# One TensorE operation for both matmuls of a scan step, and new places in the plan: a hybrid of state-space scan, convolution and attention on one core

## The chip, the cores and the metric

The kernel runs on one core of a Trainium2 chip. The metric is the device time in microseconds (us) of one execution, lower is better; the time of a kernel is the median of several runs. A separate execution was recorded by the hardware profiler, and all lines of "the profile" come from it.

## What is computed

The input x has 8 images of 384 channels by 32 x 32 pixels, so 1024 tokens each, in float32. Two layers follow each other. Cut to what matters:

```python
# layer 0: xn = rmsnorm(x); the same mamba runs forward and backward over the tokens
xz = xn @ in_proj.T;  u, z = split(xz)
u  = silu(causal_conv4(u) + b)
dt, Bm, Cm = split(u @ x_proj.T)              # rank 24, 16 states, 16 states
delta = softplus(dt @ dt_proj.T + bias)
h_t = exp(delta_t * A) * h_{t-1} + (delta_t * u_t) * Bm_t      # per channel, 16 states
y_t = sum_n h_t[n] * Cm_t[n] + D * u_t
g   = (y * silu(z)) @ out_proj.T                               # forward + backward
x   = x + res * (scale * g + sigmoid(depthwise3x3(xn)) * xn)
# layer 1, tokens of one image
t = t + attention(layernorm(t))               # 6 heads of 64, causal
t = t + gelu(layernorm(t) @ kron(..).T) @ kron(..).T           # 384 -> 1536 -> 384
```

The recurrence over h is most of the work: 384 channels x 16 states x 2 directions x 1024 tokens for each image.

## The kernel before

**The scan step.** A step handles 8 channels with their 16 states, which fill the 128 partitions, over all 1024 tokens in one direction. An image has 96 steps (`NSTEP`), eight images have 768. A step is made by `group` (L980). A DMA (L988) brings delta into a tile dA, with each channel's row repeated for its 16 states. ScalarE turns it into exp(delta*A) in place (L993). The 1024 tokens are two halves of 512, and for each half TensorE spreads delta*u over the 16 states with one bfloat16 matmul: 32 rows of the tile du3 against 32 rows of a fixed 0/1 matrix `dup` (L1002). The two halves lie in different groups of 32 rows. Each result fills one PSUM bank, a value named b. VectorE multiplies b by B in place (L1005) and runs the scan over dA and b (L1013), the second half continuing from the end of the first. GpSimd, called POOL, multiplies the state by C (L1016). `scans` (L916) lets TensorE sum two such steps over the states into a bank y, with eight records (`sums`, L950 to L959).

**Banks.** Of the eight PSUM banks, four ("psm") serve all other matmuls, three ("b") serve the scan input, and one ("y") collects the sums (`kinds`, L401). A b is free again when its scan has read it.

**The rest of the work.** For each image: `project` and `gates` make u and z, `prepare` and `deltas` make the convolution, B, C and delta, all ahead of the image's scans. Behind the scans come `local`, `finish`, `layernorm`, `attention`, `mix` and `forward`. In the middle of the run, an image's scans go on beside the preparation of later images and the attention and feed-forward of the image before.

**What sets the order.** The order on every engine is fixed before the launch by a planner, `Plan` (L105). Every operation is given with its engine, a cost in us, what it reads and writes, and a number `at`, its place. `run` (L170) plays the program through with these costs: the engine that can start earliest takes, of the operations that can start within 0.05 us of that moment, the one with the lowest place. The order found so is emitted; on the chip each engine works through its own queue strictly in it, and waits for what each instruction needs. So a place is a priority and not a time, and a cost that differs from the chip's shifts engines against each other.

- Values of kind "b" are handed out in order of place as banks come free; an operation that asks for two starts when it has both (`queue` and `hand_out`, L179 and L199).
- On ScalarE, operations whose function table is loaded are favoured by `STAY` (L247); another table costs a load, `ACT_TABLE_LOAD` in the profile. Ordinary transfers on SP wait until the planned DMA backlog is under `BACKLOG` (L238); loads with a place of their own, as the dA loads, do not.
- Scan operations get their place from the step's number, `HEAD` and `PERIOD` (L1397), with offsets: `LOAD` for the dA load, `DECAY` for the exponential, `PRODUCTS` for POOL's product, `SUMS` for y, `PARTS` for du3. The spread matmul's place, -1000 and up, comes ahead of nearly everything on TensorE.
- Other work gets places that run evenly over a window (`Window`, L446), given in periods (`PROJECT` to `FORWARD`) or in us for the first images (`PROJECT0` to `LAYER1`). Within it, VectorE and ScalarE operations that touch a psm bank are moved ahead by `EVICT`, transfers by `MOVE`.

In the profile all plain matmuls have line 331, that of the helper `mm`, so they are told apart by tile: b is the scan input, y the sums, pi the projection, pg the output projection, pk, pq and po those of attention, px and pw those of the convolutions and of B and C, s the scores. A float32 matmul leaves two records, a bfloat16 one leaves one.

Of the kernel before, what the change touches and what calls it, by code (L numbers as in the profile page):

```python
# [22 lines left out]
NH = L // HALF  # L23
# [17 lines left out]
KI, KO = 32, 12  # L41
# [38 lines left out]
def act(n):  # L80
    return 0.2 + n * 0.000833


def dve(n):
    return 0.07 + n / 940


def pool(n):
    return 0.1 + n * 0.0022
# [15 lines left out]
class Plan:  # L105
# [1 line left out]
    DRAIN = 0.19  # L107
    SLACK = 0.1
    SWITCH = 1.3
    STAY = 50.0  # L110
    BACKLOG = 50.0
    LANDING = 1.0
    DMA_LATENCY, DMA_RATE = 2.5, 262e3

# [4 lines left out]
    def op(self, engine, cost, fn, reads=(), writes=(), at=None, table=None, nbytes=0, holds=()):  # L119


        o = Op()
        o.engine, o.cost, o.fn, o.table, o.nbytes = engine, cost, fn, table, nbytes
        o.at = self.at if at is None else at
        o.placed = o.urgent = at is not None
        o.vals, o.allocs, o.users, o.ready, o.done = [], [], [], 0.0, None
        deps = set()

        def meets(a, b):
            return a is None or b is None or a == b  # L130

        for v in reads:
            v, part = v if isinstance(v, tuple) else (v, None)
            deps.update(w for w, q in v.writes if meets(part, q))
            v.reads.append((o, part))
            o.vals.append(v)
        for v in writes:
            v, part = v if isinstance(v, tuple) else (v, None)
            deps.update(w for w, q in v.writes if meets(part, q))
            deps.update(r for r, q in v.reads if meets(part, q))  # L140
            if part is None:
                v.writes, v.reads = [], []
            if v.kind is not None and v.left == 0 and v not in o.allocs:
                o.allocs.append(v)
            v.writes.append((o, part))
            o.vals.append(v)
        for v in holds:
            if v.left == 0 and v not in o.allocs:
                o.allocs.append(v)
            o.vals.append(v)  # L150
        deps.discard(o)
        o.vals = list(dict.fromkeys(o.vals))

        o.after, slot_of = [], set()
        for v in o.vals:
            v.left += 1
            if v in o.allocs:
                v.first = o
            elif v.first is not None and v.first not in deps:
                slot_of.add(v.first)  # L160
        for d in slot_of:
            d.after.append(o)
        o.waits = len(deps) + len(slot_of)
        for d in deps:
            d.users.append(o)
        o.index = len(self.ops)
        self.ops.append(o)
        return o

    def run(self):  # L170
# [55 lines left out]
        while len(order) < total:  # L226
            best = None
            for e in engines:
                cand = []
                for o in ready[e]:  # L230
# [6 lines left out]
                    if e == "SP" and not o.urgent:  # L237
                        t = max(t, dma - self.BACKLOG)  # L238
                    cand.append((max(t, free[e]), o))
# [5 lines left out]
                for t, o in cand:  # L245
                    if t <= t0 + 0.05:
                        a = o.at - (self.STAY if e == "ACT" and o.table in (None, table) else 0.0)  # L247
                        k = (a, o.index)
# [39 lines left out]
def conv_attn_hybrid_kernel(  # L288
# [41 lines left out]
    def mm(out_, lhsT, rhs, first=True, last=True):  # L330
        return nc.tensor.matmul(out_, lhsT=lhsT, rhs=rhs, start=first, stop=last)  # L331
# [6 lines left out]
    def half(hf):  # L338
        return slice(hf * HALF, (hf + 1) * HALF)
# [18 lines left out]
    dup = const.tile([P, P], BF16, name="dup")  # L358
# [51 lines left out]
    op = plan.op  # L410

    def dma(dst, src, reads, writes, nbytes, **kw):

        op("SP", 0.6, lambda: nc.sync.dma_start(dst(), src()), reads, writes, nbytes=nbytes, **kw)
# [18 lines left out]

    EVICT, MOVE, SUMS, PRODUCTS, DECAY, LOAD, PARTS = 111.21, 8.82, 26.97, -2.67, -328.02, -584.01, -478.49

    PROJECT, GATES, CONV, DELTA = (-1.521, -1.371), (-1.067, -1.026), (-0.976, -0.866), (-0.889, -0.365)
    LOCAL, OUTPUT, NORM, ATTEND = (0.661, 0.853), (1.005, 1.032), (1.082, 1.173), (1.202, 1.761)
    MIX, FORWARD = (1.787, 1.854), (1.855, 2.07)  # L440

    PROJECT0, EARLY, CONV0, DELTA0 = (-400.622, -296.945), (-523.036, 67.185), (-160.273, 70.933), (131.8, 263.184)
    GATES0, ZEROS, LATE, PROJECT1, GATES1 = (177.592, 252.86), (56.018, 117.713), (263.977, 276.95), (-19.453, 206.415), (352.446, 448.404)
    CONV1, DELTA1, LAYER1 = (250.186, 263.964), (271.922, 425.403), (675.476, 1110.704)

    class Window:  # L446

# [468 lines left out]
    def scans(b, t0, period):  # L916
# [14 lines left out]
        for a in range(NB):  # L931
            y = Val("y", [P, HALF], f"y_{b}_{a}")
            for d in range(2):
                step0 = (a * 2 + d) * GJ * BR

                du3 = Val("du3", [P, GJ, HALF], f"du3_{b}_{step0}", BF16)
                reads = [(dusd[d][s], (a // 2, k, hf)) for k in range(3) for hf in range(NH)]
                dma(
                    lambda t=du3: t.t,
                    lambda a=a, d=d: dusd[d][s].t[a * BR : (a + 1) * BR].rearrange(  # L940
                        "r h k (e j) t -> (r h k) e (j t)", j=GJ
                    ),
                    reads + [(dusd[d][s], ("z", hf)) for hf in range(NH)], [du3], P * GJ * HALF * 2, at=t0 + step0 * step_time - PARTS,
                )
                for j in range(GJ):
                    step = step0 + j * BR
                    at = t0 + step * step_time
                    hs = [group(b, a, d, j, r, at + r * step_time, du3, bcs[d]) for r in range(BR)]

                    def sums(y=y, hs=hs, d=d, j=j):  # L950
                        for hf in range(NH):
                            for r in range(BR):
                                q = hf * BR + r
                                mm(
                                    y.t[q * KI : (q + 1) * KI, :], sel[:, j].rearrange("p e i -> p (e i)"),
                                    hs[r].t[:, half(hf)], d == 0 and j == 0, d == 1 and j == GJ - 1,
                                )

                    op("PE", quad(HALF), sums, hs, [y], at=at - SUMS)  # L959
# [20 lines left out]
    def group(b, a, d, j, r, at, du3, bc):  # L980

        s = b % 2
        n = f"{b}_{a}_{d}_{j}_{r}"
        dA = Val("dA", [P, L], f"dA_{n}")

        rows = a * HC + r * KI
        src = ded[d][s].t[rows : rows + KI].rearrange("(e j) t -> j e t", j=GJ)[j]
        dma(  # L988
            lambda: dA.t, lambda: src.unsqueeze(0).to_broadcast([NS, GC, L]),
            [(ded[d][s], a // 2)], [dA], P * L * 4, at=at - LOAD,  # L990
        )
        g = (a * BR + r) * GJ + j
        op(  # L993
            "ACT", act(L) + 0.1, lambda: nc.scalar.activation(dA.t, dA.t, AF.Exp, scale=nA.t[:, g : g + 1]),  # L994
            [nA], [dA], at=at - DECAY, table=EXP,
        )
        rev = slice(None, None, -1) if d else slice(None)

        halves = [(hf, Val("b", [P, HALF], f"b_{n}_{hf}")) for hf in (range(NH - 1, -1, -1) if d else range(NH))]
        for hf, v in halves:  # L1000
            rr = slice((r * NH + hf) * KI, (r * NH + hf + 1) * KI)
            op("PE", 0.24, lambda v=v, rr=rr: mm(v.t, dup[rr, :], du3.t[rr, j]), [du3], [v], at=-1000.0 + at * 1e-3)  # L1002
        for i, (hf, v) in enumerate(halves):
            op(
                "DVE", dve(HALF), lambda v=v, hf=hf: nc.vector.tensor_mul(v.t, v.t, bc.t[:, 0, half(hf)]), [(bc, 0)], [v],  # L1005
                at=at,
            )

            def scan(v=v, hf=hf, first=i == 0):
                t = dA.t[:, half(hf)][:, rev]  # L1010

                h = 0.0 if first else dA.t[:, HALF : HALF + 1] if d else dA.t[:, HALF - 1 : HALF]
                nc.vector.tensor_tensor_scan(t, t, v.t[:, rev], h, ALU.mult, ALU.add)  # L1013

            op("DVE", 1.15, scan, [v], [dA], at=at)
        op("POOL", pool(L), lambda: nc.gpsimd.tensor_mul(dA.t, dA.t, bc.t[:, 1]), [(bc, 1)], [dA], at=at - PRODUCTS)  # L1016
        return dA
# [376 lines left out]

    PERIOD, HEAD = 393.0, 65.75  # L1397

    def stretch(span, b):
        return Window(span[0] * PERIOD, span[1] * PERIOD, HEAD + b * PERIOD)  # L1400
# [119 lines left out]
```

## Time and profile before

| | |
|---|---|
| median of 3 runs | 4003.02 us (3989.68 to 4006.04) |
| the profiled execution's own time | 4019.04 us |
| its span, first to last instruction | 4017.1 us |
| mean granted TensorE clock | 0.935 |
| instructions in the span | 54053 |
| first and last b matmul start | 151.4 us, 3742.7 us |
| moved by DMA | 858.92 MB, mean 214 GB/s |
| table loads on ScalarE | 226, 1283 ns each |

How to read it: PE is TensorE, PEld its weight loads, DVE VectorE, ACT ScalarE, POOL GpSimd, SP the engine that issues the transfers. A line of a group gives the source line, the engine, the operation, out<-in by tile, the shapes and the count; then busy us and the mean ns of one; then the engine's idle time just before, with what ended most of it. A line of waits reads: engine, tile and line, "<-", what released it, then total us, times, longest us. A timeline line gives start, duration, engine, operation and count.

### The profile page before, as it was taken

Reading aid. Unit: us, or ns where it says so; the run is one execution under the profiler, and the core shown is the slowest. Engines: PE = TensorE matmul, PEld = TensorE weight load, DVE = VectorE, ACT = ScalarE, POOL = GpSimd, SP = SyncE. Lnnn points to the kernel's source line nnn. Section 1 sums busy time; section 2 is a strip of 40 time slices with the busy share of each in tenths; the row PEclk is TensorE's granted clock in tenths of the full one; section 3 lists DMA queues with packets and bytes.
Section 4 is the critical chain, followed back from the end, with each engine's and each line's share of the span. In section 5 each row is a group of like instructions: output and inputs, shape, how many; then the busy total and the mean of one; then the engine's idle time right before and its main releaser. Section 6 shows DMA issues by size and latency. Waiting matters only on the chain.

```text
span 4017.1 us, 54053 instructions
## 1 busy us (share of the span) xinstructions
PE 3709.8 (92%) x17970; PEld 1404.8 (35%) x17970; DVE 3332.5 (83%) x4403; ACT 2825.4 (70%) x4468; POOL 2997.6 (75%) x2370
## 2 busy tenths in 40 slices
PE   7577879899999999999999999999999999999998
PEld 2111112443234432444224432444324432443363
DVE  1498979978988989889988999889998899999522
ACT  4756647776788857888678867888678867676364
POOL 1988877997579965899569975899669975776231
PEclk9677678899998999999999999989999999999998
DMA  7989997679976898769976799669986698578100
GB/s 249 270 243 262 255 258 218 178 225 239 270 213 179 236 238 259 205 187 251 269 232 199 226 253 285 190 185 255 260 242 194 181 255 240 147 192 218 49 20 25
DMA packets 301998, 858.92 MB, mean 214 GB/s; under 512 B 38312, under 2 KB 91576, under 8 KB 301720
## 3 DMA queue, kind: packets, MB, share of 16 engines
q1 hardware_dynamic: 301720, 855.47, 76.4%
q8 instruction: 143, 2.34, 0.3%
q14 instruction: 135, 1.11, 0.1%
HBM read 696.44 MB, written 160.68 MB: 213 GB/s over the span
## 4 chain that ended last, share of the span: by engine, by line
PE 53%; DVE 14%; DMA 10%; POOL 8%; issue 4%; ACT 2%; SPq 0%; POOLq 0%; DVEq 0%; ACTq 0%
DVE dA L1013 7%; PE b L331 7%; PE pc L331 6%; PE y L331 5%; PE pi L331 4%; DMA dA<-ded 4%; POOL dA L1016 4%; DVE b L1005 3%; PE t L1250 3%; PE s L331 3%; PE pk L331 3%; PE pvv L331 3%; PE pq L331 2%; DVE mx L1186 2%; POOL p L1240 2%
## 5 line engine op out<-in xcount | busy, mean ns | idle before, releaser
L1016 POOL TENSOR_TENSOR dA<-dA,bc 128x1024 f32<-128x1024 f32 x768 | 1806.1, 2363 | 605.0 <-DVE dA L1013 506.4
L1013 DVE TENSOR_TENSOR_SCAN dA<-dA,b 128x512 f32<-128x512 f32 x1536 | 1854.3, 1234 | 92.7 <-ACT dA L994 90.3
L1005 DVE TENSOR_TENSOR b<-b,bc 128x512 f32<-128x512 f32 x1536 | 996.9, 681 | 173.2 <-PE b L331 161.4
L994 ACT ACTIVATE dA<-dA,nA 128x1024 f32<-128x1024 f32 x768 | 863.4, 1145 | 272.3 <-DMA dA<-ded 234.0
L331 PE MATMUL b<-du,dup 32*128 32x512 bf16 x1536 | 609.4, 408 | 181.0 <-DVE dA L1013 158.8
L331 PE MATMUL y<-dA,sel 128*32 128x512 f32 x3072 | 489.2, 663 | 11.2 <-POOL dA L1016 8.3
L331 PEld LDWEIGHTS <-dup 32*128 32x128 bf16 x1536 | 132.9, 92 | 935.4 <-issue 903.0
L1186 DVE TENSOR_REDUCE mx<-s 128x1 f32<-128x512 f32 (+3 forms) x576 | 288.7, 547 | 186.1 <-PE s L331 182.3
L1240 POOL TENSOR_SCALAR p<-p,den 128x512 f32<-128x512 f32 (+3 forms) x576 | 327.1, 586 | 86.0 <-DVE den L1232 79.3
L1193 ACT ACTIVATE p<-s,mx 128x512 f32<-128x512 f32 (+3 forms) x576 | 329.4, 578 | 75.0 <-DVE mx L1186 74.1
L1257 ACT COPY pT<-t 128x512 f32<-128x512 f32 (+2 forms) x480 | 245.9, 546 | 129.2 <-PE t L1250 123.1
L331 PE MATMUL pi<-xp,win 128*128 128x512 f32 x576 | 312.4, 650 | 10.4 <-DVE xp L696 4.5
L1250 PE MATMUL t<-ident,p 128*128 128x128 f32 x1728 | 281.6, 298 | 29.7 <-POOL p L1240 14.0
L1456 ACT ACT_TABLE_LOAD x226 | 290.0, 1283 | 4.0
L331 PE MATMUL s<-k,q 64*128 64x512 f32 (+3 forms) x1152 | 283.7, 544 | 9.2 <-ACT p L1193 8.6
L1250 PEld LDWEIGHTS t<-ident,p 128*128 128x128 f32 x1728 | 200.1, 149 | 164.8 <-issue 74.0
L331 PE MATMUL pc<-pT,v 128*64 128x128 f32 x3456 | 251.0, 289 | 5.3 <-ACT pT L1257 4.9
L331 PEld LDWEIGHTS pc<-pT,v 128*64 128x64 f32 x3456 | 193.9, 142 | 100.5 <-ACT pT L1257 31.2
L913 POOL TENSOR_TENSOR u<-u,part 128x1024 f32<-128x1024 f32 x96 | 204.9, 2134 | 10.5 <-ACT part L905 9.9
L905 ACT CAST part<-u 128x1024 bf16<-128x1024 f32 x144 | 150.5, 1045 | 64.8 <-DMA dusd<-part 49.9
L1365 ACT ACTIVATE g<-ph 128x512 f32<-128x512 f32 x192 | 104.1, 595 | 118.4 <-PE ph L331 117.4
L331 PEld LDWEIGHTS y<-dA,sel 128*32 128x32 f32 x3072 | 75.4, 112 | 286.2 <-issue 152.6
(184 smaller groups left out, 4776.1 us busy)
## 6 DMA issues: line engine op xcount, KB each, us to landing
dA<-ded SPq DMA_DIRECT2D x768, 512.0 KB
ct<-urd SPq DMA_DIRECT2D x96, 513.5 KB
du<-dusd SPq DMA_DIRECT2D x96, 512.0 KB
xs<-xpd SPq DMA_DIRECT2D x96, 432.8 KB
dusd<-part SPq DMA_DIRECT2D x288, 128.0 KB
ded<-de SPq DMA_DIRECT2D x48, 512.0 KB
uz<-uzd SPq DMA_DIRECT2D x48, 512.0 KB
bc<-bcd SPq DMA_DIRECT2D x32, 512.0 KB
```

Source lines behind the costliest of these rows:

```text
L331: return nc.tensor.matmul(out_, lhsT=lhsT, rhs=rhs, start=first, stop=last)
L913: "POOL", pool(L), lambda part=part: nc.gpsimd.tensor_sub(du.t, du.t, part.t), [part], [du]
L994: "ACT", act(L) + 0.1, lambda: nc.scalar.activation(dA.t, dA.t, AF.Exp, scale=nA.t[:, g : g + 1]),
L1005: "DVE", dve(HALF), lambda v=v, hf=hf: nc.vector.tensor_mul(v.t, v.t, bc.t[:, 0, half(hf)]), [(bc, 0)], [v],
L1013: nc.vector.tensor_tensor_scan(t, t, v.t[:, rev], h, ALU.mult, ALU.add)
L1016: op("POOL", pool(L), lambda: nc.gpsimd.tensor_mul(dA.t, dA.t, bc.t[:, 1]), [(bc, 1)], [dA], at=at - PRODUCTS)
L1186: lambda sc=sc, g=g, w=k1 - k0, hh=hh: nc.vector.tensor_reduce(mx.t[:, g, hh : hh + 1], sc[hh].t[:, 0:w], AX.X, ALU.max, negate=True), [sc ...
L1193: nc.scalar.activation(ps[g].t[:, hh, 0 : k1 - k0], sc[hh].t[:, 0 : k1 - k0], AF.Exp, bias=mx.t[:, g, hh : hh + 1], accum_out=den.t[:, g, ...
L1240: nc.gpsimd.tensor_scalar(t, t, den.t[:, g, hh : hh + 1], 1.0, ALU.mult, ALU.mult)
L1250: nc.tensor.transpose(t.t[:, o + j * P : o + (j + 1) * P], ps[g].t[:, hh, j * P : (j + 1) * P], ident)
L1257: nc.scalar.copy(pT[g].t[:, hs[0] : hs[-1] + 1, 0:w], t.t[:, 0 : len(hs) * w].rearrange("p (h w) -> p h w", w=w))
L1456: nc.scalar.preload_act_table_set(table)
```

## The change

In `group`, the two matmuls that fill a step's two b banks were two planner operations of cost 0.24, each with one bank. They become one operation of cost 0.336 that issues both matmuls one after the other and takes both banks when it starts. It keeps its place. The readers on VectorE stay as they are.

All hand-set places and three of the planner's settings get other numbers: `STAY`, `BACKLOG`, the seven offsets, all windows, `PERIOD` and `HEAD`.

```diff
@@ class Plan
-    STAY = 50.0
-    BACKLOG = 50.0
+    STAY = 15.0
+    BACKLOG = 10.0
@@
-    EVICT, MOVE, SUMS, PRODUCTS, DECAY, LOAD, PARTS = 111.21, 8.82, 26.97, -2.67, -328.02, -584.01, -478.49
+    EVICT, MOVE, SUMS, PRODUCTS, DECAY, LOAD, PARTS = 27.83, 13.24, 12.22, -9.17, -222.27, -783.55, -339.2
-    PROJECT, GATES, CONV, DELTA = (-1.521, -1.371), (-1.067, -1.026), (-0.976, -0.866), (-0.889, -0.365)
-    LOCAL, OUTPUT, NORM, ATTEND = (0.661, 0.853), (1.005, 1.032), (1.082, 1.173), (1.202, 1.761)
-    MIX, FORWARD = (1.787, 1.854), (1.855, 2.07)
+    PROJECT, GATES, CONV, DELTA = (-1.525, -1.398), (-1.067, -0.985), (-0.952, -0.894), (-0.917, -0.358)
+    LOCAL, OUTPUT, NORM, ATTEND = (0.593, 0.969), (1.016, 1.081), (1.16, 1.227), (1.191, 1.755)
+    MIX, FORWARD = (1.81, 1.845), (1.879, 2.092)
-    PROJECT0, EARLY, CONV0, DELTA0 = (-400.622, -296.945), (-523.036, 67.185), (-160.273, 70.933), (131.8, 263.184)
-    GATES0, ZEROS, LATE, PROJECT1, GATES1 = (177.592, 252.86), (56.018, 117.713), (263.977, 276.95), (-19.453, 206.415), (352.446, 448.404)
-    CONV1, DELTA1, LAYER1 = (250.186, 263.964), (271.922, 425.403), (675.476, 1110.704)
+    PROJECT0, EARLY, CONV0, DELTA0 = (-373.152, -337.008), (-788.581, -96.07), (-84.26, 78.46), (50.858, 257.144)
+    GATES0, ZEROS, LATE, PROJECT1, GATES1 = (253.962, 443.889), (24.114, 455.177), (161.216, 306.444), (-92.709, 246.406), (452.944, 585.724)
+    CONV1, DELTA1, LAYER1 = (164.85, 479.335), (392.72, 578.245), (462.639, 791.646)
@@ def group
-        for hf, v in halves:
-            rr = slice((r * NH + hf) * KI, (r * NH + hf + 1) * KI)
-            op("PE", 0.24, lambda v=v, rr=rr: mm(v.t, dup[rr, :], du3.t[rr, j]), [du3], [v], at=-1000.0 + at * 1e-3)
+
+        def spread():
+            for hf, v in halves:
+                rr = slice((r * NH + hf) * KI, (r * NH + hf + 1) * KI)
+                mm(v.t, dup[rr, :], du3.t[rr, j])
+
+        op("PE", 0.336, spread, [du3], [v for _, v in halves], at=-1000.0 + at * 1e-3)
@@
-    PERIOD, HEAD = 393.0, 65.75
+    PERIOD, HEAD = 418.62, 167.66
```

## The prediction

> **What bounds the kernel now.** I read the page's busy line and its costliest groups first, then busy time by stages, then VectorE's waits, then single stretches of TensorE's timeline.
>
> ```profile
> PE 3709.8 (92%) x17970; PEld 1404.8 (35%) x17970; DVE 3332.5 (83%) x4403; ACT 2825.4 (70%) x4468; POOL 2997.6 (75%) x2370
> ...
> L1013 DVE TENSOR_TENSOR_SCAN dA<-dA,b 128x512 f32<-128x512 f32 x1536 | 1854.3, 1234 | 92.7 <-ACT dA L994 90.3
> L1005 DVE TENSOR_TENSOR b<-b,bc 128x512 f32<-128x512 f32 x1536 | 996.9, 681 | 173.2 <-PE b L331 161.4
> ...
> L331 PE MATMUL b<-du,dup 32*128 32x512 bf16 x1536 | 609.4, 408 | 181.0 <-DVE dA L1013 158.8
> ```
>
> The matmul that the change pairs is 609 of TensorE's 3710 us. Its reader, the product and the scan on VectorE, is the largest work of that engine: 2 x (0.681 + 1.234) = 3.83 us for each of the 768 steps.
>
> By stages (the span cut where the scans start, at 151 us, end, at 3745 us, and in eight equal parts between, one for each image):
>
> ```profile
> core 0: us, PE busy (x) PEld busy (x) DVE busy (x) ACT busy (x) POOL busy (x), PEclk, DMA share, GB/s
> 151.00:600.00 449.00, 333.54 (x1065) 68.54 (x1067) 390.92 (x453) 258.85 (x272) 386.01 (x188) 0.69 0.93 260
> ...
> 1948.00:2397.00 449.00, 435.40 (x2231) 168.34 (x2231) 408.78 (x535) 348.90 (x554) 369.95 (x291) 0.99 0.83 233
> ...
> 3295.00:3745.00 450.00, 428.42 (x2168) 160.98 (x2168) 438.31 (x575) 297.06 (x487) 300.13 (x253) 0.98 0.72 189
> 3745.00:4017.00 272.00, 253.66 (x1334) 127.81 (x1333) 73.82 (x145) 131.23 (x331) 59.10 (x147) 0.96 0.09 32
> ```
>
> Four kinds of stretch: the first image is held by transfers (DMA share 0.93, TensorE only 74% busy), the six in the middle by TensorE (97%), the last image's scans by VectorE (97%), and the tail by TensorE alone. Over the six middle images (600 to 3295 us, 449.2 each) TensorE is busy 2591 us and VectorE 2411: 432 and 402 an image.
>
> Whether a busy TensorE is a full one has to be asked. The Trainium skill (Perfetto Trace Analysis, Identifying the Most-Contended Engine) holds that matmul busy time is a bad measure, and that weight-load busy share is a better one. By that, the middle windows stand at 168/449 = 37%, TensorE has room, and the change would give next to nothing. I checked by start times instead: between 600 and 3295 us, all time by which two matmul starts lie further apart than 0.54 us sums to 107 us, 4%. Its queue issues almost without pause. Here the trace decides: TensorE is the bound, and what an instruction costs is the distance it puts between its neighbours' starts.
>
> **What a lone matmul costs.** Two stretches of TensorE's timeline:
>
> ```profile
> 2000.40 1.12 PE L331 MATMUL pg<-yg,wout 128*128 128x512 f32 x2
> 2001.45 0.39 PE L331 MATMUL b<-du,dup 32*128 32x512 bf16 x1
> 2001.77 1.98 PE L331 MATMUL pg<-yg,wout 128*128 128x512 f32 x4
> 2003.69 0.39 PE L331 MATMUL b<-du,dup 32*128 32x512 bf16 x1
> ```
>
> ```profile
> 1876.40 1.07 PE L331 MATMUL pw<-xs,wl__13047 96*32 96x512 f32 x8
> 1877.40 0.39 PE L331 MATMUL b<-du,dup 32*128 32x512 bf16 x2
> 1877.72 1.07 PE L331 MATMUL pw<-xs,wl__13047 96*32 96x512 f32 x8
> ```
>
> In the first, every b sits alone; the next instruction starts 0.32 us after it, and the stretch before it is longer too. Where a lone b stands between two matmuls of one kind, their starts are 0.84 us apart (pi, pg, pk, po, pq, px: 208 cases), and without it 0.43 (pg, pk, po, px) or 0.53 (pi, pq). So a lone b costs 0.31 to 0.41 us; I take 0.36. In the second stretch two b's stand together: they share one 0.39 us and the next starts 0.32 us after. Their rows differ, and the second starts 3 to 37 ns after the first. A second b beside the first is nearly free. Of 1377 runs of b's, 1291 have only one, and only 27 neighbours start together.
>
> **The change, part by part.**
>
> *The pair.* 768 - 27 = 741 lone matmuls go from TensorE's path: 741 x 0.36 = 267 us (230 to 304 at the ends). An image has 96 steps, so TensorE falls from 432 to about 432 - 741/8 x 0.36 = 399 us, level with VectorE's 402, whose work does not change. So VectorE takes over, and the gain is counted from its idle time.
>
> ```profile
> DVE mx L1186 <- PE s L331: 94.7, 80, 8.2
> DVE dA L1013 <- ACT dA L994: 81.9, 35, 11.1
> DVE b L1005 <- PE b L331: 57.7, 74, 3.3
> DVE x L1319 <- PE po L331: 12.0, 12, 3.0
> ```
>
> These are VectorE's waits over the six middle images (total us, times, longest). TensorE's lateness is the first, third and fourth, with smaller ones 175 us, 29 us an image. ScalarE's and the transfers' lateness is 82 + 17 = 99 us, 16.5 an image, which the pair doesn't touch.
>
> *What remains of TensorE's lateness.* The nearest row is the last scan window: there TensorE is 95% busy, VectorE 97%, and the same two waits (mx on s, b on b) are 3.5 and 2.4 us. I take 5 us an image, between none and the 29 of now.
>
> *The wait that is added.* There are three b banks. Now the second-to-come b takes the spare one early, and a bank need be refilled only two halves later. The pair is placed where two banks are free, so after the scan of the earlier half of the step before; from there VectorE has one more scan, 1.24 us, until it wants the pair. Behind a pair that waits for its bank stand, in order on TensorE, the y sums and all of attention; ahead of a late one stands at most one indivisible operation, about 1.0 us (y's eight records). Cost from both sides: below, a TensorE with room ends the present 57.7 us of b waits, 0.08 us a step, a gain already counted above; above, 1.0 + 0.36 - 1.24 = 0.12 us in each step if the operation ahead always has all to run, more where the order and real times drift apart (now b starts a median 0.5 to 0.8 us after its bank is free, so the drift is of that size). I take 0.05 us a step, 5 us an image; up to 0.5 for the range. The Trainium skill (TensorEngine Tiling, Gotcha 1: PSUM Pressure) speaks against the change here: row tiles go to different banks and so press on PSUM. By the rule the price is the pair holding two of three banks, by the row it is the 0.12 us that the 1.24 us scan leaves uncovered; I follow the row.
>
> *The new places.* No row shows the new order. EVICT 111 to 28 ranks evictions less early; STAY 50 to 15 lets ScalarE change tables more readily (226 loads of 1.283 us now, 290 us); BACKLOG 50 to 10 holds ordinary transfers back so that a dA load meets a shorter queue; the rest shifts work of one image against another. The plan's own price for the pair (0.336) is close to the 0.36 of the trace, while its 0.24 for one was not: the order should fit the chip better. Ends: a gain of at most the 99 us of ScalarE's and the transfers' lateness; a loss of about 108 us if table loads double (another 290 us, 36 us an image on an engine at 345 of 449, half of it late for a scan, over six images). I take nothing. SP issues the same number of transfers. The head (151 us), the first image, the last image's scans and the tail I leave as they are: none is held by b except in the first, where TensorE idles anyway.
>
> **The sum.** A middle image: 402 (VectorE) + 16.5 (ScalarE, transfers) + 5 (TensorE late) + 5 (pair) = 428.5 us against 449.2, a gain of 20.7, times six = 124 us. From the profiled execution, 4019 us (span 4017.1 and 2 us around it), that leaves 3895, 3.1% less. It ran 0.4% over the median of the runs shown; the same share of 4003 gives 3880.
>
> **The rivals.**
>
> 1. *The pair's bank wait outweighs it (slower).* If TensorE blocks at the pair, or VectorE waits for it, at every step, the gain of 267 us is used up at 267/768 = 0.35 us a step. Place: b's wait on the scan. At 0.5 us the sum is (0.5 - 0.35) x 768 = 115 us over, 4118. For it: banks are few, and VectorE, now with slack in the middle, would have none; in the first image TensorE already waits 108 us for b's banks. Against: in the middle it waits only 36 us, 65 times. With the loss from the places, I give slower 27%.
>
> 2. *Hidden anyway (same).* Transfers at 0.81 share, POOL at 0.82 and ScalarE's lateness refill what TensorE gives up, as they hold the first image now: 4003. For it: the longest pieces of the ending chain are POOL and DMA pieces of 9 to 18 us. Against: the last scan window ran VectorE at 97%. 12%.
>
> 3. *The ceiling.* VectorE reaches the last window's 97.4% in all six: 402/0.974 = 413, gain 36 x 6 = 217 us, 3787, or lower if the transfers' lateness goes as well. 14%.
>
> That the pair doesn't run side by side is excluded by the second timeline above, which has it.
>
> **How the numbers follow.** Likeliest, 47%: 3880, its own range 3800 to 3965. With the ceiling, faster by over 0.5% has 61%, within 0.5% (about what a measurement of this kernel can tell from no change) 12%, slower 27%. The range reaches to 3770, below the ceiling's figure, and up to 4090, short of the rival's 4118: some 6% lie below and 12% above.
>
> **What would show it.** Right: b's 1536 records busy near 320 us, nearly all starting in twos; TensorE's busy in the middle windows near 93% and VectorE's near 94%; VectorE's wait on s well under 95 us; b on b no more than about 60. Wrong: TensorE's wait on the scan before b in the hundreds; VectorE waiting for dA's exponentials far longer than 82 us; table loads far above 226; a tail or head that grew.

## The result, and the profile after

The changed kernel takes 3945.02 us (median, 3941.6 to 3957.49), the kernel before 4003.02: a ratio of 0.9857, 95% interval 0.9836 to 0.9878. It is faster by 1.4%, where 3.1% was forecast: 58 us of 123.

The profiled execution after has a span of 3939.9 us, 77 less than before's; it ran 3 us under its kernel's median and before's 16 us over, so 19 of the 77 are the spread between executions. From the costliest groups of its page:

```profile
L1017 DVE TENSOR_TENSOR_SCAN dA<-dA,b 128x512 f32<-128x512 f32 x1536 | 1906.1, 1242 | 36.4 <-ACT dA L994 18.1
L1009 DVE TENSOR_TENSOR b<-b,bc 128x512 f32<-128x512 f32 x1536 | 986.3, 683 | 166.7 <-PE b L331 160.6
...
L331 PE MATMUL b<-du,dup 32*128 32x512 bf16 x1536 | 412.9, 407 | 218.8 <-DVE dA L1017 160.4
```

The b matmul went from 609 to 413 us of busy TensorE, not to some 320. And the scan, which nobody touched, is busy 1906 us instead of 1854.

The middle of the run is best cut by the scans themselves: from the first scan of the second image to the first scan of the eighth, each 192 scans being taken as one image. Before:

```profile
560.30:3325.70 2765.40, 2641.89 (x13271) 1018.66 (x13271) 2478.67 (x3239) 2086.11 (x3307) 2237.32 (x1740) 0.96 0.82 227
```

After:

```profile
534.80:3260.80 2726.00, 2538.70 (x13308) 1009.56 (x13308) 2500.26 (x3241) 2087.98 (x3308) 2251.19 (x1747) 0.95 0.84 234
```

The columns are the stretch, its length, then PE, PEld, DVE, ACT and POOL busy, the granted TensorE clock, the DMA share and GB/s. Six images take 2726 instead of 2765 us: 39 us, or 6.6 an image, where 20.7 was forecast. TensorE's busy time fell by 103 us, VectorE's rose by 22. The other 38 us of the span: 3 in the head, 23 in the first image, 2 in the last one's scans, 10 in the tail.

The chain that ended last did move to VectorE, as forecast. Its shares of the span by engine, before and after:

```profile
PE 53%; DVE 14%; DMA 10%; POOL 8%; issue 4%; ACT 2%; SPq 0%; POOLq 0%; DVEq 0%; ACTq 0%
```

```profile
DVE 33%; PE 25%; DMA 15%; POOL 12%; issue 7%; ACT 7%; SPq 1%; POOLq 0%; DVEq 0%; ACTq 0%
```

VectorE's waits after, in this stretch:

```profile
DVE mx L1190 <- PE s L331: 78.9, 42, 7.6
DVE b L1009 <- PE b L331: 48.8, 38, 6.6
DVE xr L1108 <- ACT pv_a L336: 38.7, 11, 6.8
DVE dA L1017 <- ACT dA L994: 11.7, 6, 4.5
```

Before, in the same stretch, they were 94.7, 57.9, 8.3 and 81.9 us. The two waits for TensorE fell little, although TensorE is freer; all of VectorE's waits for TensorE add up to 132 us in the middle, against 175 before. The wait for the exponentials, which the pair was not to touch, fell by 70 us, and a wait in the layer norm grew by 30.

What became of the pair shows in a stretch of TensorE's and VectorE's timeline after (start, duration; count at the end):

```profile
1632.74 1.79 PE L331 MATMUL s<-k,q 64*128 64x512 f32 x4
1633.06 1.28 DVE L1009 TENSOR_TENSOR b<-b,bc 128x512 f32<-128x512 f32 x2
...
1634.32 2.52 DVE L1017 TENSOR_TENSOR_SCAN dA<-dA,b 128x512 f32<-128x512 f32 x2
1634.47 0.38 PE L331 MATMUL b<-du,dup 32*128 32x512 bf16 x1
1635.58 0.37 PE L331 MATMUL b<-du,dup 32*128 32x512 bf16 x1 [0.72 <-DVE dA L1017]
1635.88 0.92 PE L331 MATMUL s<-k,q 64*128 64x384 f32 x4
```

Two things are to be seen. The first b of the pair starts at 1634.47 in the spare bank; the second waits until the scan begun at 1634.32 has given back its bank, and the scores stand behind it for 1.1 us. Some 480 of the 768 pairs start together. And the two scans take 2.52 us: they are the halves of one step. Before, two scans in a row were mostly of different steps (350 times in the middle, against 49 of one step; after, 17 against 357):

```profile
2110.49 2.38 DVE L1013 TENSOR_TENSOR_SCAN dA<-dA,b 128x512 f32<-128x512 f32 x2
```

Over the middle, the second of two such scans starts a median 1.188 us behind the first in the kernel before, 1.245 us in the changed one.

TensorE's granted clock changed too, from 0.96 to 0.95 in the two lines of the middle. The trace holds two grants, full and half. In the middle TensorE stood at half clock for 212 us before and for 270 after, and it was busy for 182 and 234 us of these. Two neighbouring stretches after, at half and at nearly full clock, and the same eight records of y in each:

```profile
2693.50:2700.30 6.80, 6.80 (x25) 1.66 (x24) 6.72 (x11) 5.25 (x11) 6.72 (x9) 0.50 1.03 245
2700.30:2707.00 6.70, 6.68 (x58) 3.45 (x60) 6.63 (x9) 5.44 (x14) 6.62 (x12) 0.99 1.03 256
```

```profile
2696.40 1.93 PE L331 MATMUL y<-dA,sel 128*32 128x512 f32 x8
2700.27 1.08 PE L331 MATMUL y<-dA,sel 128*32 128x512 f32 x8
```

At half clock the same work takes nearly twice as long, so about half of the busy time there is lost. By that, 26 us of the 52 by which it grew is my estimate of what TensorE lost again to its clock.

### The profile page after: what moved, and what is told of

It is laid out like the page before. It is cut to its first block, busy times and chain, and to the rows that moved or that the text cites. A ratio compares the mean times of both kernels' runs of the same rounds, so it can differ in the third digit from the quotient of the medians.

```text
span 3939.9 us, 54075 instructions
## 1 busy us (share of the span) xinstructions
PE 3545.6 (90%) x17970; PEld 1386.8 (35%) x17970; DVE 3362.0 (85%) x4403; ACT 2821.3 (72%) x4465; POOL 2999.4 (76%) x2370
## 4 chain that ended last, share of the span: by engine, by line
DVE 33%; PE 25%; DMA 15%; POOL 12%; issue 7%; ACT 7%; SPq 1%; POOLq 0%; DVEq 0%; ACTq 0%
DVE dA L1017 20%; DVE b L1009 7%; DMA dA<-ded 5%; POOL dA L1020 5%; PE t L1254 3%; PE pc L331 3%; PE y L331 2%; PE s L331 2%; PE pq L331 2%; POOL p L1244 2%; PE b L331 2%; DVE mx L1190 2%; DMA dusd<-part 1%; DMA yg<-ygd 1%; PE pi L331 1%
## 5 line engine op out<-in xcount | busy, mean ns | idle before, releaser
L1017 DVE TENSOR_TENSOR_SCAN dA<-dA,b 128x512 f32<-128x512 f32 x1536 | 1906.1, 1242 | 36.4 <-ACT dA L994 18.1
L1009 DVE TENSOR_TENSOR b<-b,bc 128x512 f32<-128x512 f32 x1536 | 986.3, 683 | 166.7 <-PE b L331 160.6
L331 PE MATMUL b<-du,dup 32*128 32x512 bf16 x1536 | 412.9, 407 | 218.8 <-DVE dA L1017 160.4
L331 PE MATMUL s<-k,q 64*128 64x512 f32 (+3 forms) x1152 | 302.7, 552 | 20.3 <-ACT p L1197 18.4
L1261 ACT COPY pT<-t 128x512 f32<-128x512 f32 (+1 forms) x480 | 245.5, 547 | 96.1 <-PE t L1254 87.9
L331 PE MATMUL pi<-xp,win 128*128 128x512 f32 x576 | 300.3, 640 | 13.9 <-ACT de L887 6.3
L331 PEld LDWEIGHTS <-dup 32*128 32x128 bf16 x1536 | 76.6, 92 | 593.9 <-issue 572.3
L1254 PEld LDWEIGHTS t<-ident,p 128*128 128x128 f32 x1728 | 208.3, 152 | 204.7 <-POOL p L1244 123.9
L331 PEld LDWEIGHTS s<-k,q 64*128 64x128 f32 x1152 | 110.5, 191 | 176.2 <-ACT p L1197 72.8
```

The source lines that it names most:

```text
L1254: nc.tensor.transpose(t.t[:, o + j * P : o + (j + 1) * P], ps[g].t[:, hh, j * P : (j + 1) * P], ident)
L1261: nc.scalar.copy(pT[g].t[:, hs[0] : hs[-1] + 1, 0:w], t.t[:, 0 : len(hs) * w].rearrange("p (h w) -> p h w", w=w))
```

## The experiments

All ratios are to the kernel before, measured beside the run on the same chip, with 95% intervals. Its medians there were 4001 to 4012 us. A difference in us between two of the other kernels is mostly one between different chips.

**Half of the change (e1, e2).** e1 has the pair with all places and settings of before; e2 has all new places and settings, with two single matmuls.

> The kernel before, with the pair alone; all places and settings as before. Theory A (the pair relieves TensorE by about 267 us but its second half blocks TensorE while it waits for its bank, and the places are neutral): about the time of the changed kernel, 3930 to 3960, with the in-pair distance of starts adding up to 100 us or more. Theory B (the gain comes from the places, the shorter wait for dA among them, and the pair alone brings nothing): 3990 to 4020. Theory C (the pair is worth the forecast 124 us and the new places give half back): about 3880.

> The kernel before with all new places and settings, but two single matmuls per step as before. Theory A: 3990 to 4020, as before. Theory B: about 3945. Theory C: slower than before, 4040 or more. VectorE's wait for dA's exponentials should fall from 82 us to near 12 in the middle if the settings alone shorten it.

e1: 4017.87 us, 1.0052 (1.0021 to 1.0082). e2: 4013.01 us, 1.0048 (1.0023 to 1.0073). Each half alone is no faster (half a per cent slower, which is less than another order moves the time, below), both together are 1.4% faster; none of the three theories had both. VectorE's wait for the exponentials was 55 us in e1's middle and 105 in e2's, so the new settings alone don't shorten it. The in-pair distances of starts add up to 146 us in e1's middle, as the blocking theory has it, and 148 in the changed kernel's.

**Relief of one engine in the unchanged order (e3, e8, e14, e15, e13).** The planner runs with before's costs, so the order is before's on every engine; each kernel leaves a part of the computation out.

```diff
 # e3, in accumulate
-                mm(*args(), first, last)
+                if not (i == 1 and not last and p.name[:3] in ("pi_", "pq_", "pk_", "po_", "pg_")):
+                    mm(*args(), first, last)
 # e8, the product before the scan
-nc.vector.tensor_mul(v.t, v.t, bc.t[:, 0, half(hf)])
+nc.vector.tensor_mul(v.t[:, 0:344], v.t[:, 0:344], bc.t[:, 0, half(hf)][:, 0:344])
 # e14
-nc.scalar.activation(dA.t, dA.t, AF.Exp, scale=nA.t[:, g : g + 1])
+nc.scalar.activation(dA.t[:, 0:592], dA.t[:, 0:592], AF.Exp, scale=nA.t[:, g : g + 1])
 # e15
-nc.gpsimd.tensor_mul(dA.t, dA.t, bc.t[:, 1])
+nc.gpsimd.tensor_mul(dA.t[:, 0:864], dA.t[:, 0:864], bc.t[:, 1, 0:864])
 # e13: the load fills columns 0:512 of dA; the exponential reads them for both halves
-lambda: dA.t, lambda: src.unsqueeze(0).to_broadcast([NS, GC, L]),
+lambda: dA.t[:, 0:HALF], lambda: src[:, 0:HALF].unsqueeze(0).to_broadcast([NS, GC, HALF]),
```

> The kernel before in exactly its order and with single matmuls; TensorE leaves out the middle one of three terms in the sums pi, pq, pk, po and pg (one third of the channels is left out of these projections), about 270 us of its work, as much as the pair should free. No bank wait is added and nothing is moved. Theory A (blocking is what cost the rest): the full forecast or more, 3880 or lower. Rival D (in a fixed order the other engines hold the pace, so that relief of TensorE is worth only some 60 us however it is got): 3930 to 3960.

e3: 3988.98 us, 0.9956 (0.9932 to 0.9979), a gain of 14 us. This falls short of both theories, and it is the most telling run of the study: TensorE had as much work less as the pair was to save. Where it went, in e3's waits on TensorE and VectorE in the middle:

```profile
PE b L331 <- DVE dA L1014: 146.7, 209, 6.4
```

```profile
DVE mx L1187 <- PE s L331: 86.9, 68, 7.4
DVE dA L1014 <- ACT dA L995: 82.4, 36, 10.1
DVE b L1006 <- PE b L331: 51.3, 57, 3.2
```

TensorE's busy time in the middle fell from 2642 to 2518 us; its wait at b rose from 54 to 147, and VectorE's waits stayed. A TensorE busy 96% was not what held the pace alone. Two limits of this run: over the whole span 564 records are gone, some 270 us at the distances of the prediction, but the busy time fell only from 3710 to 3534 us, and part of the difference went to the clock (half clock for 282 us of the middle, against 212; mean grant 0.917 against 0.935). And this relief lies in the projections and not in every scan step as the pair's does; one spread like the pair's, without its bank wait, was not tried.

> The kernel before in exactly its order; the product before each scan covers 344 of the 512 columns (a third of the tokens of each half are left without the factor B), 0.18 us less in each of 1536, about 275 us of VectorE's work. Theory F (VectorE and the waits on its path hold the pace also where TensorE is the busiest): 3750 to 3850. Rival G (in a fixed order no single engine holds it, as the relief of TensorE by as much gave 14 us): 3960 or more. In between: a pace held in turn.

e8: 3985.11 us, 0.9934 (0.9911 to 0.9957), 26 us of 275, in the range of rival G; VectorE's wait on b in the middle rose from 58 to 130 us.

> The kernel before in exactly its order; the exponential covers 592 of 1024 columns (the decay of the other tokens is left as delta itself), 0.36 us less in each of 768, about 276 us of ScalarE's work. If ScalarE holds the pace: 3850 or lower. If not: within 30 us of before, 3970 to 4005.

> The kernel before in exactly its order; POOL's product covers 864 of 1024 columns (C is left out for the others), about 0.36 us less in each of 768, some 270 us of POOL's work. POOL is busy 82% of the middle and ends the chain of many long pieces. If POOL holds the pace: 3850 or lower. If not: 3970 to 4005.

e14: 4010.61 us, 1.0008 (0.9981 to 1.0034). e15: 4014.3 us, 1.0004 (0.9974 to 1.0034). Within the 0.3% of these intervals, neither ScalarE's exponentials nor POOL's products hold anything by their length.

> The kernel before in exactly its order, but each dA load brings only the first 512 of 1024 tokens, and the exponential uses them for both halves (delta of the second half of the tokens is left out). That halves 393 of the 859 MB moved. If the transfers and the late dA hold the pace: 3850 or lower, and VectorE's wait for the exponentials (82 us in the middle) near none. If they don't: 3960 to 4000.

e13: 3959.93 us, 0.988 (0.9837 to 0.9923), 51 us. Two of its waits between 556 and 3290 us, one on ScalarE and one on VectorE:

```profile
ACT dA L994 <- DMA dA<-ded: 32.1, 11, 6.1
```

```profile
DVE dA L1016 <- ACT dA L994: 80.9, 33, 11.1
```

Before, these were 176.5 and 81.9 us. The loads come in time, and the exponentials are still late for VectorE. In e13 ScalarE's longest waits are for TensorE's results in attention and the feed-forward (pT, cT and g, 231 us together); that an exponential is late because it stands behind those in ScalarE's queue fits, but was not tried; nor is it settled where e13's 51 us come from.

**Several reliefs at once (e9, e17).** e9 joins e3 and e8; e17 joins e3, e8 and e13.

> The kernel before in exactly its order, with both reliefs at once: TensorE leaves out a third of the terms of pi, pq, pk, po and pg (some 270 us), VectorE's product covers 344 of 512 columns (some 275 us). Theory H (TensorE and VectorE hold each other in lock step through b, y and s, so that only both together free the time): 3850 or lower, far below the 14 and 27 us that each gave alone. Rival I (the rest is held outside both, by the late loads of dA and the order of the transfers): 3940 to 3975, about the sum of the two.

> The kernel before in exactly its order with three reliefs at once: a third of the terms of pi, pq, pk, po and pg left out on TensorE (some 270 us), the product on VectorE over 344 of 512 columns (some 275 us), half the bytes of the dA loads (the second half of the tokens uses the first half's delta). If the three hold the pace in turn and hide each other: far more than the sum of their single gains (89 us), 3800 or lower. If the fixed order itself holds it, each engine waiting in its queue for others that wait in theirs: about the sum, 3900 to 3930.

e9: 3956.03 us, 0.9867 (0.9822 to 0.9912), 47 us, about the sum of the two, as rival I had it. e17: 3825.38 us, 0.9571 (0.9538 to 0.9604), 176 us, about twice the sum of the three alone (14 + 26 + 51 = 91); it lies between its two expected ranges, nearer to the first. So more than one of TensorE, VectorE and the loads hold the pace in turn, and what one gives up the others take back. The loads belong to it: their relief gives 129 us on top of e9's and gave 51 alone. Whether TensorE does is less sure: VectorE and the loads without TensorE were not tried.

**VectorE's own price of the pair (e10).** The changed kernel in its own order, without the carry.

```diff
-h = 0.0 if first else dA.t[:, HALF : HALF + 1] if d else dA.t[:, HALF - 1 : HALF]
+h = 0.0
```

> The changed kernel in exactly its order, but the scan of a step's second half starts from zero instead of from the end of the first half (the carry over the middle of the sequence is left out). In the changed kernel, two scans in a row are always the halves of one step, and the second start lies 1.245 us after the first instead of 1.188. Theory J (the pair made VectorE's own work longer by this dependence): VectorE's busy time in the six middle images falls from 2500 to about 2470 us, and the time by 10 to 30 us. Rival (the longer scans lie in time that VectorE would wait anyway): 3935 to 3950.

e10: 3918.61 us, 26 us under the changed kernel's 3945, as theory J had it, and 0.9787 (0.9749 to 0.9825) to before. The page's row of its scans:

```profile
L1017 DVE TENSOR_TENSOR_SCAN dA<-dA,b 128x512 f32<-128x512 f32 x1536 | 1807.5, 1204 | 22.2 <-ACT dA L994 20.1
```

This takes away more than the pair added: 99 us of scan time off the 1906, while the pair's addition is about 50. The busy row of the scan is 1854 to 1858 us in every kernel with single matmuls and 1903 to 1906 in every one with the pair and the carry. If the gain goes with the relief, some 13 of the 26 us are the pair's; that is an estimate.

**Less blocking at the pair (e4).** The planner is given the durations of the profile.

```diff
-"DVE", dve(HALF), lambda v=v, hf=hf: nc.vector.tensor_mul(...)
+"DVE", 0.684, lambda v=v, hf=hf: nc.vector.tensor_mul(...)
-op("DVE", 1.15, scan, [v], [dA], at=at)
+op("DVE", 1.24, scan, [v], [dA], at=at)
```

> The changed kernel, but the planner is given the times that the profile shows for the scan (1.24 instead of 1.15) and for the product before it (0.684 instead of 0.615). Theory A (TensorE comes to the pair too early, because the plan takes the scan for shorter than it is, and blocks on its second bank): in-pair waits fall to half or less of the 148 us that the changed kernel shows in its six middle images, and the time falls to 3880 to 3920. Rival (any re-ordering moves the time by as much in either direction): no link between in-pair waits and time.

e4: 4037.2 us, 1.0093 (1.0071 to 1.0116). The in-pair distances fell from 148 to 82 us, and the time rose, by 92 us over the changed kernel's. The first half of theory A came, the second did not. TensorE's wait for POOL's products before y rose from 4 to 43 us. The profile's durations in the plan cut the blocking and made a worse order, so the run cannot say what the blocking costs. What it shows is that another order of the same pair and places can cost 2.4%.

**How far the order itself moves the time (e5, e6, e7, e11, e12, e16, e18).** A change of 0.2 in `PERIOD` (before: 393.0; after: 418.62) is meant to give another order and nothing else. e7 changes `HEAD` by 0.5. e18 is the pair with before's places and only `STAY = 15.0`, `BACKLOG = 10.0`.

> The kernel before with PERIOD 393.2 instead of 393.0, 0.05% more, nothing else. The order that the planner finds differs nearly everywhere from then on. Theory E (the hand-set places pick one order out of many that lie some tens of us apart, and each kernel's places were good for its own operations only): 20 to 60 us slower, 4025 to 4065. Rival (the places as such make the time, so a change this small leaves it): 3995 to 4010.

> The changed kernel with PERIOD 418.82 instead of 418.62, 0.05% more, nothing else. Theory E: 20 to 60 us slower, 3965 to 4005, which would be most or all of the change's gain. Rival (pair and places as such make the gain): 3935 to 3955.

> The changed kernel with HEAD 168.16 instead of 167.66, half a us in the places of all scans, nothing else. Theory E: 3965 to 4005. Rival: 3935 to 3955.

> The pair with the places of before, PERIOD 393.2 instead of 393.0: a second draw of an order for this combination. If the pair is worth something in itself, clearly below the 4040 that the single matmuls gave with this same PERIOD: 3990 to 4020. If not, 4025 to 4055.

> Single matmuls with the new places, PERIOD 418.82: a second draw. If the new settings are worth something in themselves, below 4040: 4000 to 4025. If not, 4025 to 4055. The pair with these very places and this PERIOD took 3975.

> The kernel before with PERIOD 392.8 instead of 393.0. If 4003 was a good draw of the plan, this lies near the 4040 that PERIOD 393.2 gave, 4020 to 4060. If 393.2 was a bad draw: 3990 to 4015.

> The pair with all hand-set places of before, and only STAY 15 and BACKLOG 10 of the new settings. If these two let the pair give its time: 3940 to 3975. If the hand-set places do: 4000 to 4035, as the pair with all of before's settings (4018 and 4008).

| | as given | PERIOD + 0.2 | another |
|---|---|---|---|
| single, old places | 1 | e5: 4039.76, 1.0083 (1.0063 to 1.0103) | e16, PERIOD - 0.2, nearly before's order: 4015.34, 1.0007 (0.9984 to 1.0029) |
| pair, old places | e1: 1.0052 | e11, e1's order: 4008.06, 1.0014 (0.9995 to 1.0033) | e18, new settings: 4084.79, 1.0211 (1.0182 to 1.024) |
| single, new places | e2: 1.0048 | e12: 4031.8, 1.007 (1.0049 to 1.009) | |
| pair, new places | 0.9857 | e6: 3974.88, 0.992 (0.9889 to 0.995) | e7, HEAD + 0.5: 3957.69, 0.9877 (0.9857 to 0.9897) |

Not all of these are different orders. Going through VectorE's rows in the trace one by one, another tile stands in 38% of the places in e5 (against before), 50% in e12 (against e2), 49% in e6 and 48% in e7 (against after). In e16 it is 2%, and in e11, against e1, none: the planner gave the same order on every engine. So e1 and e11 are one order measured twice, on two chips, and their 1.0052 and 1.0014 show how well a time repeats. And e16 is hardly a second draw: that 4003 was a lucky draw of the old plan, as e5 suggested, it does not refute.

A change without meaning moves a kernel by up to 0.8%, more than half of the change. Yet with the planner's costs as they are, the three orders with the pair and the new places are faster than every other kernel here that computes everything (e4, with other costs, is slower than before). The pair under the old places shows no gain in its one order with the old settings, nor do the new places without it in two. Of the two settings alone, e18 says that they don't bring the gain; with places that don't fit them they cost 2%.

## Why the prediction was wrong

The direction was right, the size was wrong by half, and the direction was in part luck: the sum put the whole gain down to the pair, which alone brought none (e1), and took the new places at nothing, without which there is none.

The step that failed is the one after the view by stages: "the trace decides: TensorE is the bound", and with it "VectorE takes over, and the gain is counted from its idle time". I took the engine busy 96% for the one that holds the pace, and let VectorE's waits for TensorE fall from 29 us an image to 10 (5 that remain, 5 for the pair). They fell to 22, from 175 to 132 us over the six images. e3 took 124 us of busy time from TensorE in the middle, more than the 103 of the pair, and collected 14 us. An engine in a fixed queue is busy 96% and still waits at the right moments: relieved, it waits longer for VectorE's scans, and VectorE waits as before. The measure that the prediction set aside, 37% by the weight loads and so next to no gain, came nearer to e1 and e3. Rival 2, that others refill what TensorE gives up, named the right mechanism, but as transfers and POOL; e15 excludes POOL's length, e13 and e17 show the loads as one part.

By the terms of the sum:

- *The pair's saving, 267 us.* b fell by 196 us of busy time. The second matmul is nearly free where both start together, as the trace of before showed; but some 290 of 768 pairs don't.
- *TensorE's relief, 33 us an image.* Its busy time fell by 17. In the middle b gave 156 us (445 to 290), the other matmuls took back 53, about half of it at the lower clock. The sum had no term for the clock. What that costs in time was not tried apart.
- *The added wait, 5 us an image.* I sought it at VectorE, where the wait on b went from 57.9 to 48.8 us as forecast. It came on TensorE, inside the pair: neighbouring b's start 148 us apart in sum in the middle, against 49 before, 17 us an image. Not all of this is new waiting: TensorE's idle time before b, while VectorE still worked, rose only from 64 to 83 us, since lone b's had waited too. The rest is the second matmul's own time, which those pairs don't save.
- *"VectorE's work does not change."* It rose by 22 us in the middle. A pair that takes two of three banks lets VectorE run only step by step, with the two dependent scans in a row. I had reckoned with the banks and not with VectorE's order. Worth about 13 us by the estimate at e10.
- *VectorE's 402 us an image.* I cut the six images from equal eighths of the scan time. By the scans themselves they take 461 us, not 449, with 413 of VectorE's work. The remaining idle time was right (48), the ceiling 11 us too low.
- *The wait on s, "well under 95".* 78.9.
- *The new places, taken at nothing.* They are worth nothing alone (e2, e12), but without them the pair shows no gain either: it is at 1.0052 and 1.0014 in its one order under the old places, where the single matmuls are at 1 and, in e5's order, at 1.0083. Under the new places the pair is 1.5% to 1.9% faster than the single matmuls (e6 against e12, the changed kernel against e2). The wait for the exponentials fell from 82 to 12 us, which I had put at the end of the range. The first image gained 23 us and the tail 10, which I had left as they were.

What stays open: why pair and new places need each other. The exponentials are in time only with both (VectorE waits 82 us for them before, 55 in e1, 105 in e2, 12 after), but that is a trace, not a test, and e7, nearly as fast as the changed kernel, waits 44. A good draw of the order is a rival that three orders make unlikely and do not exclude, since e4 keeps the pair and the places and is slower than before. And that the in-pair blocking costs time was not shown: e4 changed the order with it. A fourth b bank was not tried.

No version that computes everything beat the changed kernel.

## What to carry to other kernels

In a kernel whose engines run fixed, interlocked queues, a busy share of 96% does not make an engine the bound: cut its work in the unchanged order first, and see how much of it comes back, before counting a saving as time. When a change takes several buffers at once, look at what it does to the order of the reader: here two scans that had been of different steps became dependent neighbours. And where a planner sets the order, compare several orders of each version, moved by a meaningless amount, before a per cent is put down to the edit, and make sure that the orders do differ: two of the three small changes to the old plan here gave nearly or exactly the order that they were to replace. Last, look at the clock of an engine that was relieved: here TensorE stood at half clock for 270 us of the middle instead of 212.

## What the runs showed of the hardware

In the trace of before, a scan of 128 x 512 that follows an independent one starts 1.188 us after it, about 0.08 us before the other's recorded end; in the changed kernel's, one that takes its first value from the scan just before it starts 1.245 us after, 0.036 us past its end. Without the carry, two scans in a row start 1.127 us apart (e10), so reading the carry costs something even where nothing waits: all scans average 1204 ns then, against 1242. And a lone 32-row bfloat16 matmul of 512 columns puts 0.31 to 0.41 us between full-height float32 ones, the same as two side by side (0.843 between the neighbours' starts after, 0.840 before). Where the granted clock was 0.50 instead of 0.99, eight records of y took 1.93 us instead of 1.08.
